# A graph layer and an attention layer on one core: attention and scores of a group of four samples as one block in every second step

## The chip, the cores and the metric

The kernel runs on one NeuronCore of a Trainium2 chip. Five engines run their own instruction streams and meet at semaphores: TensorE (PE; its weight loads are listed apart as PEld), VectorE (DVE), ScalarE (ACT), GpSimd (POOL), and SyncE (SP), which here issues the DMAs. The metric is device time in microseconds of one execution. Three executions gave 1952.86, 1950.43 and 1951.32 us, median 1951.32.

## The reference

The input `x` is 128 samples of 128 nodes by 512 features, and `adj` is a 128 x 128 matrix of weights. Cut to what matters (names shortened):

```python
# layer 0, per sample
A = adj @ x                       # with W1 = W2 = adj the difference C - A is the bias b alone
x = layernorm(x + max_n relu(A[:, n] + b))         # one number per node, added to its row
# layer 1, per sample: 8 heads of 64
q, k, v = split(x @ w_qkv)
p = softmax(where(adj == 0, -inf, q @ k.T / 8))
o = (p @ v) @ w_proj + b_proj
x = layernorm(x + o + layernorm(o) * gamma + beta)
```

All of it is float32. The only mask is `adj`, the same for all samples and heads.

## The kernel before

**Tiling.** The 128 samples are 64 pairs and 32 groups of four (`G = 4`). The products with the large weights are made per group, 512 tokens at once, as *units* (class `Unit`): `qk_unit(g, 0)` and `qk_unit(g, 1)` give the transposed queries and keys of two halves of the heads, `v_unit(g)` the values, `o_unit(g)` the output projection. A unit is a fast 2 x 2 block multiplication with seven products instead of eight: `product(i)` issues four fp32 matmuls of 128x128 by 128x256 (each is two MATMUL records in the trace, so a product is a row of x8), `snap(k)` copies bank 1 to SBUF on ACT, and `result(half, col)` adds a bank and a snap on DVE into the unit's output. `result(h, c)` reads bank 3 with snap 3 (1,1), bank 4 with snap 3 (1,0), bank 2 with snap 1 (0,0) and bank 3 with snap 2 (0,1). The sums of operands that the method needs run on POOL (`x_sums`, `o_sums`, `run_sums`).

**PSUM.** Eight banks, each one tag: b1 to b4 belong to the unit at work (products 1, 6, 7 share b1; 5 and 3 share b3; 2 has b2; 4 has b4); `po`, `pa`, `pss0`, `pss1` serve the attention, the scores and layer 0's product with `adj`.

**Per sample.** `scores(b)` (L396) makes eight small matmuls of 64 rows, even and odd heads into two banks. `softmax_max(b)` (L407) scales and masks each bank on DVE into a tile `s` and takes the negated maxima `nmax`. `softmax_exp` (L425) is one ACT activation per head with its sum. `softmax_div` and `prob_transpose` (L439, L447) run on DVE. `prob_write` (L457) sends the 32x32-transposed probabilities to DRAM, and `prob_read` (L466, four DMAs) fetches them back as the transposed tile `pT`. `attend(b)` (L482) makes eight small matmuls of 64 columns from `pT` and the values, and `attend_copy` (L496) takes the result to `oT` on ACT.

**The loop.** `for p in range(LAST)` (L810, `LAST = 60`) handles one pair of samples per step and two units per step: even steps (`ph == 0`) do `qk_unit(g + 1, 0)` and `o_unit(g - 1)`, odd ones `qk_unit(g + 1, 1)` and `v_unit(g + 1)`. Every step from the second on begins with `attend` of the two samples of the step before and `scores` of its own two, in one stretch of small matmuls between two units. Beside that, a step carries layer 0 for a later pair (`l0_norm`, `l0_transpose`, `l0_write`, `l0_read`, `l0_mm`, `l0_max`, `l0_add`), and the tails of earlier pairs (`tail_bias`, `tail_inner`, `tail_residual`, `tail_outer`, `tail_store`), whose row statistics `bn` computes on DVE (`one("o", ...)`, `one("z", ...)`, `one("y", ...)`) and `finish_stats` ends on POOL. After the loop the last four steps are written out by hand (from L983).

**What sets the order.** Every instruction is pinned (`pin = tc.keep_in_program_order`), so each engine executes its instructions in the order of the source; there is no planner. A tile's tag and `bufs` say how many buffers it rotates through: a new tile waits until the readers of the one whose buffer it takes are done. The SP queue issues DMAs in source order too, and one that has to wait holds those behind it.

Of the kernel before, what the change touches and what calls it, by code (L numbers as in the profile page):

```python
# [16 lines left out]
def kernel(  # L17
# [10 lines left out]
    out: bass.AP,  # L28
):


# [18 lines left out]
    H = 8  # L50
    HD = D // H
    KC = D // P
    G = 4
# [258 lines left out]
    def l0_transpose(q):  # L312

        xts[q] = sb.tile([P, Q, KC, 2, QS], F32, tag="xt", name=f"xt_{q}", bufs=2)
        for j in range(2):
            pin(
                nc.vector.transpose(  # L317
                    xts[q][:, :, :, j].rearrange("p q c b -> p c q b"),
                    xs[2 * q + j].rearrange("p (c q a) -> p c q a", c=KC, q=Q),
                )  # L320
            )
# [50 lines left out]
    def qk_unit(g, q):  # L372
        for h in range(2):
            qk[g, q, h] = sb.tile(
                [P, 2, 2, HT], F32, tag=f"qk{h}", name=f"qk_{g}_{q}_{h}", bufs=2 + h
            )
        out = {(h, c): qk[g, q, h][:, c] for h in range(2) for c in range(2)}
        return Unit(f"qk_{g}_{q}", x_lefts[g], weight_stationary(wqk, 2 * q * P), out)

    def v_unit(g):  # L380
        for h in range(2):
            vs[g, h] = sb.tile([P, 2, D], F32, tag="v", name=f"v_{g}_{h}", bufs=2)
        out = {(h, c): vs[g, h][:, :, ds(c * HE, HE)] for h in range(2) for c in range(2)}
        return Unit(f"v_{g}", x_lefts.pop(g), tokens_stationary(wv), out)
# [21 lines left out]

    def softmax_max(b):  # L407
        s = sb.tile([P, 2, NP, P], F32, tag="s", name=f"s_{b}", bufs=2)
        for par in range(2):
            pin(  # L410
                nc.vector.scalar_tensor_tensor(  # L411
                    s[:, par],
                    pss[b][par],
                    SCALE,
                    mask.unsqueeze(1).to_broadcast([P, NP, P]),
                    ALU.mult,
                    ALU.add,
                )
            )
        del pss[b]  # L420
        prob[b] = s.rearrange("p a h m -> p (a h) m")
        nmax[b] = small.tile([P, H], F32, tag="nmax", name=f"nmax_{b}")
        pin(nc.vector.tensor_reduce(nmax[b], prob[b], AX.X, ALU.max, negate=True))  # L423
# [42 lines left out]
    def prob_read(b):  # L466
        hop = hops.pop(b)
        pT[b] = sb.tile([P, Q, H, QS], F32, tag="pT", name=f"pT_{b}", bufs=2)
        for q in range(Q):
            pin(  # L470
                nc.sync.dma_start(
                    out=pT[b][ds(q * QS, QS)].rearrange("a i h b -> a i (h b)"),
                    in_=hop[:, :, q].rearrange("i a f -> a i f"),
                )
            )
# [144 lines left out]
    def z_tile(b):  # L620
        q, j = divmod(b, 2)
        tag, bufs = {58: ("xt", 2), 59: ("xt", 2), 60: ("z", 1), 61: ("qk0", 2)}.get(q, ("xs", 1))
        if tag == "xs":
# [182 lines left out]
    def tails(p):  # L806
        return [q if q >= 0 else None for q in (p - 3, p - 4, p - 5)]

    LAST = B // 2 - 4
    for p in range(LAST):  # L810
        g, ph = divmod(p, 2)
        a, b = 2 * p, 2 * p + 1
        first = v_unit(0) if p == 0 else qk_unit(g + 1, ph)
        n = p + 4 if p + 4 < B // 2 else None
        f = p + 5 if p + 5 < B // 2 else None
# [4 lines left out]
        def one(kind, src, q):  # L820
            for t in (2 * q, 2 * q + 1):
                bn(src[t], mv, len(keys))
                keys.append((kind, t))

        if p > 0:
            attend(a - 2)
            before.snap(3)
            attend_copy(a - 2)
            attend(b - 2, "pa")
            attend_copy(b - 2)  # L830
            scores(a)
            scores(b, ("po", "pa"))
        else:
            before.snap(3)
        before.result(1, 1)
        if ph == 0 and p > 0:
            run_sums(xsums[2:3])
        if ph == 0 and ta is not None:
            tail_bias(ta)
        if ph == 0 and g > 0:  # L840
            sums = o_sums(g - 1)
            run_sums(sums[:3])
        if n is not None and p > 0:
            for j in range(2):
                l0_norm(2 * n + j)
        if tb is not None:
            tail_inner(tb)
        if p > 0:
            softmax_max(a)
        before.result(1, 0)  # L850
        if p > 0:
            softmax_max(b)
            first.product(1)
            first.snap(1)
            first.product(2)
            softmax_exp(a)
        else:
            first.product(2)
            first.product(1)
            first.snap(1)  # L860
            for j in range(2):
                l0_norm(2 * n + j)
        first.result(0, 0)
        before.product(3)
        before.result(0, 1)
        if ph == 0 and p > 0:
            run_sums(xsums[3:])
        if ph == 0 and g > 0:
            run_sums(sums[3:])
        if tb is not None:  # L870
            tail_residual(tb)
        if n is not None:
            l0_transpose(n)
            l0_write(n)
            l0_beta(n)
        if ph == 1 and ta is not None:
            tail_bias(ta)
        first.product(6)
        if p == 0:
# [5 lines left out]
            softmax_exp(a)  # L885
        else:
            softmax_exp(b, range(4))
            first.snap(2)
            softmax_exp(b, range(4, H))
        first.product(5)  # L890
        first.product(4)
        first.product(7)
        if p == 0:
            first.snap(3)
            softmax_exp(b)
        softmax_div(a)
        prob_transpose(a)
        prob_write(a)
        if n is not None:
            l0_read(n)  # L900
        if p > 0:
            first.snap(3)
        else:
            first.result(1, 1)
            first.result(1, 0)
# [4 lines left out]
        prob_read(b)  # L910
        if p > 0:
            first.result(1, 1)
            first.result(1, 0)
        if ph == 1 and tb is not None:
            one("z", zs, tb)
        if ph == 0 and ta is not None:
            one("o", o_rows, ta)
        if f is not None:
            for j in range(2):
                l0_mm(2 * f + j, f"pss{j}")  # L920
        if to is not None:
            tail_outer(to)
            tail_store(to)
        if n is not None:
            l0_spill(n)
        if ta is not None:
# [11 lines left out]
        second.snap(1)  # L938
        if f is not None:
            for j in range(2):  # L940
                l0_max(2 * f + j)
                l0_add(2 * f + j)
        first.product(3)
        first.result(0, 1)
        if ph == 0 and tb is not None:
            one("z", zs, tb)
        if ph == 1 and ta is not None:
            one("o", o_rows, ta)
        second.product(6)
        second.snap(2)  # L950
        second.product(5)
        second.result(0, 0)
        second.product(4)
# [3 lines left out]
        if p == 1:  # L957
            weight_sums(wp, 0, HE)
            bd = const.tile([P, HE], F32, name="bd")
            tt(nc.gpsimd, bd, bp_bc[:, HE:], bp_bc[:, :HE], ALU.subtract)  # L960
        if f is not None:
            one("y", xs, f)
# [4 lines left out]
        before = second  # L967


# [14 lines left out]
    keys = []  # L984
    attend(L - 9)
    before.snap(3)
    attend_copy(L - 9)
    attend(L - 8, "pa")
    attend_copy(L - 8)
    scores(L - 7)  # L990
    scores(L - 6, po_pa)
    before.result(1, 1)
# [4 lines left out]
    tail_inner(LQ - 7)  # L997
    softmax_max(L - 7)
    before.result(1, 0)
    softmax_max(L - 6)  # L1000
    first.product(1)
    first.snap(1)
    first.product(2)
    softmax_exp(L - 7)
    first.result(0, 0)
    before.product(3)
    before.result(0, 1)
    run_sums(xsums[3:])
    run_sums(sums[3:])
    tail_residual(LQ - 7)  # L1010
    first.product(6)
    scores(L - 5)
    scores(L - 4, po_pa)
    softmax_exp(L - 6, range(4))
    first.snap(2)
    softmax_exp(L - 6, range(4, H))
    first.product(5)
# [3 lines left out]
    softmax_max(L - 5)  # L1021
    first.snap(3)
    prob_out(L - 6)
    first.result(1, 1)
    prob_read(L - 7)
# [30 lines left out]
    second.product(7)  # L1056
    prob_out(L - 4)

# [6 lines left out]
    attend(L - 6, "pa")  # L1065
    attend_copy(L - 6)
    prob_read(L - 5)
    prob_read(L - 4)
    before.result(1, 1)
    before.result(1, 0)  # L1070
    o_u.product(1)
# [16 lines left out]
    softmax_max(L - 3)  # L1088
    softmax_max(L - 2)
    o_u.product(6)  # L1090
    o_u.snap(2)
# [10 lines left out]
    o_u.result(1, 1)  # L1102
    o_u.result(1, 0)
    softmax_max(L - 1)
    stats("last_1", ("o", L - 9), ("o", L - 8))
# [7 lines left out]
    softmax_exp(L - 1, range(4, H))  # L1113
    v_u.relayed()
    softmax_max(L)
    for t in (L - 9, L - 8):
# [158 lines left out]
```

## Time and profile before

| what | value |
|---|---|
| profiled execution, device time | 1951.72 us |
| its span (first to last instruction) | 1949.8 us |
| PE busy | 1936.3 us, 99% of the span |
| DVE, POOL, ACT busy | 1564.1, 1293.1, 1063.7 us (80%, 66%, 55%) |
| PE clock granted | 0.999 |
| DMA | 341.74 MB, mean 175 GB/s |
| start of one step's small matmuls to the next | 29.97 us (1003.34 to 1033.31 to 1063.28) |

The page gives each engine's busy time, then the chain of work that ended last, followed back from the last instruction: at each step to what released it, or to the instruction before it on its engine. The timeline lists merged stretches of equal instructions of an engine: start, length, engine, line, operation, output and inputs, shapes, count, and in brackets an idle time before it and what ended it. The length runs from the first start to the last end; as matmuls are pipelined, an end lies up to 0.27 us (small ones) or 0.38 us (128x256) after the record's start, and the rate is read from starts.

### The profile page before, as it was taken

What the parts mean: (1) busy time and instruction counts of PE and PEld (TensorE: products, weight loads), DVE (VectorE), ACT (ScalarE), POOL (GpSimd) and SP (SyncE); (2) the same over time, 40 slices, a digit from 0 to 9 for tenths busy, and PEclk for the clock granted to TensorE, in tenths of its full rate; (3) what the DMA queues carried; (4) which work ended last, traced back from release to release, by engine and by line L of the source; (5) the groups of instructions that cost most, each with busy time, mean ns of one, the idle gap of its engine ahead of it and who ended that gap; (6) DMA issues with size and microseconds to landing.
All of it is one profiled execution on the core that took longest, in us unless ns stands there. A gap on an engine that the chain in (4) does not pass through costs nothing.

```text
span 1949.8 us, 33046 instructions
## 1 busy us (share of the span) xinstructions
PE 1936.3 (99%) x11541; PEld 1641.8 (84%) x11541; DVE 1564.1 (80%) x2515; ACT 1063.7 (55%) x3094; POOL 1293.1 (66%) x823
## 2 busy tenths in 40 slices
PE   9999999999999999999999999999999999999998
PEld 6888888888888888888888888888888888888885
DVE  7767878778778787787887877877878778778787
ACT  3444655555546555555465555554655555546566
POOL 6436766768667676667676676766767666767648
PEclk9999999999999999999999999999999999999999
DMA  7747566576576665766766757657667576675564
GB/s 221 176 119 192 141 186 176 161 205 159 167 195 159 187 176 167 199 157 171 203 152 183 182 160 199 163 166 195 157 185 191 156 195 164 166 206 152 157 226 141
DMA packets 444934, 341.74 MB, mean 175 GB/s; under 512 B 276832, under 2 KB 378336, under 8 KB 444768
## 3 DMA queue, kind: packets, MB, share of 16 engines
q1 hardware_dynamic: 444336, 338.85, 64.5%
q8 instruction: 91, 1.49, 0.3%
q10 hardware_dynamic: 432, 0.79, 0.1%
q14 instruction: 75, 0.61, 0.1%
HBM read 172.82 MB, written 166.72 MB: 174 GB/s over the span
## 4 chain that ended last, share of the span: by engine, by line
PE 94%; DVE 3%; POOL 1%; ACT 1%; issue 0%; POOLq 0%; ACTq 0%; DVEq 0%
PE b_qk L74 39%; PE b_v L74 19%; PE b_o L74 18%; PE pss L74 6%; PE po L74 6%; PE pa L74 5%; DVE st_mv_last L261 0%; POOL zl L77 0%; DVE s_x L77 0%; ACT s L430 0%; POOL s_o L77 0%; DVE amax L297 0%; PE idle L74 0%; DVE xt L317 0%; DVE mv_last L262 0%
## 5 line engine op out<-in xcount | busy, mean ns | idle before, releaser
L74 PE MATMUL b_qk<-s_x,wqk 128*128 128x256 f32 x2048 | 473.7, 380 | 1.0 <-DVE qk L77 0.7
L74 PEld LDWEIGHTS b_qk<-s_x,wqk 128*128 128x128 f32 x2048 | 389.8, 191 | 54.7 <-DVE qk L77 1.4
L430 ACT ACTIVATE s<-s,nmax 128x128 f32<-128x128 f32 x1024 | 396.0, 390 | 5.3 <-DVE nmax L423 5.3
L74 PE MATMUL b_qk<-x1T,wqk 128*128 128x256 f32 x1536 | 359.0, 384 | 1.1 <-DVE x1T L329 1.0
L74 PEld LDWEIGHTS b_qk<-x1T,wqk 128*128 128x128 f32 x1536 | 287.5, 190 | 45.3 <-POOL wqk L77 1.2
L77 POOL TENSOR_TENSOR z<-z,ga_bc 128x1024 f32<-128x1024 f32 x58 | 164.6, 2838 | 167.1 <-ACT z L284 167.1
L275 POOL TENSOR_SCALAR rs_mv<-mv 128x6 f32<-128x6 f32 (+2 forms) x61 | 14.7, 241 | 386.0 <-DVE mv L262 386.0
L77 DVE TENSOR_TENSOR s<-s,rec 128x1024 f32<-128x1024 f32 x128 | 252.6, 1973 | 4.4
L186 ACT COPY u_qk<-b_qk 128x512 f32<-128x512 f32 x192 | 112.3, 585 | 238.5 <-PE b_qk L74 237.5
L74 PE MATMUL b_v<-wv,s_x 128*128 128x256 f32 x1024 | 237.1, 380 | 0.0
L74 PE MATMUL b_o<-wp,s_o 128*128 128x256 f32 x992 | 229.6, 380 | 0.2 <-ACT u_o L186 0.2
L74 PEld LDWEIGHTS b_v<-wv,s_x 128*128 128x128 f32 x1024 | 195.0, 191 | 26.3 <-ACT u_v L186 0.4
L411 DVE SCALAR_TENSOR_TENSOR s<-pss,mask 128x512 f32<-128x512 f32 x256 | 164.4, 684 | 61.1 <-PE pss L74 60.9
L74 PEld LDWEIGHTS b_o<-wp,s_o 128*128 128x128 f32 x992 | 188.8, 191 | 25.8 <-issue 0.8
L77 DVE TENSOR_TENSOR qk<-b_qk,u_qk 128x512 f32<-128x512 f32 x256 | 168.0, 675 | 48.9 <-PE b_qk L74 44.5
L77 POOL TENSOR_TENSOR x<-x,be_bc 128x1024 f32<-128x1024 f32 x64 | 182.1, 2847 | 30.8 <-DVE rec L441 27.4
L430 ACT ACTIVATION_READ_ACCUMULATOR s<-s,nmax 128x1 f32 x1024 | 193.5, 189 | 0.0
L77 DVE TENSOR_TENSOR v<-b_v,u_v 128x512 f32<-128x512 f32 x127 | 86.2, 680 | 131.5 <-PE po L74 128.8
L186 ACT COPY u_o<-b_o 128x512 f32<-128x512 f32 x91 | 53.3, 585 | 239.6 <-PE b_o L74 239.6
L186 ACT COPY u_v<-b_v 128x512 f32<-128x512 f32 x95 | 55.6, 585 | 234.3 <-PE b_v L74 234.3
L74 PE MATMUL b_v<-wv,x1T 128*128 128x256 f32 x768 | 176.5, 380 | 0.0
L74 PEld LDWEIGHTS b_v<-wv,x1T 128*128 128x128 f32 x768 | 146.3, 191 | 31.8 <-issue 13.6
(130 smaller groups left out, 3402.9 us busy)
## 6 DMA issues: line engine op xcount, KB each, us to landing
hop<-pu SPq DMA_DIRECT2D x128, 512.0 KB, 3.6
pT<-hop SPq DMA_DIRECT2D x512, 128.0 KB, 3.6
spill<-x SPq DMA_DIRECT2D x64, 512.0 KB, 4.7
x<-in_x_dram SPq DMA_DIRECT2D x62, 512.0 KB, 4.2
xhop<-xt SPq DMA_DIRECT2D x248, 128.0 KB, 2.3
x1T<-xhop SPq DMA_DIRECT2D x248, 128.0 KB, 3.9
xr<-spill SPq DMA_DIRECT2D x59, 512.0 KB, 3.3
out_dram<-xr SPq DMA_DIRECT2D x58, 512.0 KB, 4.0
```

The lines of the kernel that those rows point to most:

```text
L74: pin(nc.tensor.matmul(*args, **kwargs))
L77: pin(eng.tensor_tensor(dst, a, b, op))
L186: pin(nc.scalar.copy(t, self.banks[1]))
L275: pin(nc.gpsimd.tensor_scalar(rs[:, :n], mv[:, :n, 1], EPS, None, ALU.add))
L411: nc.vector.scalar_tensor_tensor(s[:, par], pss[b][par], SCALE, mask.unsqueeze(1).to_broadcast([P, NP, P]), ALU.mult, ALU.add,)
L430: nc.scalar.activation(prob[b][:, i], prob[b][:, i], AF.Exp, bias=nmax[b][:, i : i + 1], accum_out=psums[b][:, i : i + 1],)
```

## The change

The change touches the loop's order and a few buffers; no instruction is added or removed on any engine.

- `group_block(old)` puts the attention of four samples (two in step 2) and the scores of the next four into one stretch at the start of each even step from step 2 on. Odd steps from 3 on have no such stretch. The four attentions use `po`, `pa`, `pss0`, `pss1`; the scores use b2 and b1, then b4 and `po`, then `pa` and `pss0`, then `pss1` and b2.
- `softmax_max` is split: `softmax_mask` does the masking, and can be called ahead. `group_mask` masks all four samples of a group in the even step, the last one's second bank first. The maxima of the third sample are taken at the end of the even step, those of the fourth early in the odd step.
- `v` has four buffers instead of two, `qk1` two instead of three, `xt` one instead of two (with one `xt` tile in `z`'s buffer). `s` and `pT`, two each before, share one tag with four.
- In odd steps the results of the unit before come ahead of most else on DVE, exponentials of the third sample's first half run first on ACT, and those of the fourth sample's second half after the unit's last snap.
- In even steps the maxima of layer 0 (`l0_first`) and the statistics move behind the unit's second snap, and `second.result(0, 0)` comes ahead of the statistics of `z`.
- In the hand-written end the first block takes four attentions and four scores as well, `prob_out(L - 4)` moves into the next block, and the last two samples are masked into spare room of the weight buffer.

```diff
-        xts[q] = sb.tile([P, Q, KC, 2, QS], F32, tag="xt", name=f"xt_{q}", bufs=2)
+        tag = "z" if q == 3 else "xt"
+        xts[q] = sb.tile([P, Q, KC, 2, QS], F32, tag=tag, name=f"xt_{q}", bufs=1)
...
-                [P, 2, 2, HT], F32, tag=f"qk{h}", name=f"qk_{g}_{q}_{h}", bufs=2 + h
+                [P, 2, 2, HT], F32, tag=f"qk{h}", name=f"qk_{g}_{q}_{h}", bufs=2
...
-            vs[g, h] = sb.tile([P, 2, D], F32, tag="v", name=f"v_{g}_{h}", bufs=2)
+            vs[g, h] = sb.tile([P, 2, D], F32, tag="v", name=f"v_{g}_{h}", bufs=4)
...
-    def softmax_max(b):
-        s = sb.tile([P, 2, NP, P], F32, tag="s", name=f"s_{b}", bufs=2)
-        for par in range(2):
+    def softmax_mask(b, order=(0, 1), place=None):
+        s = place or sb.tile([P, 2, NP, P], F32, tag="s", name=f"s_{b}", bufs=4)
+        for par in order:
...
+    def softmax_max(b):
+        if b in pss:
+            softmax_mask(b)
...
-        pT[b] = sb.tile([P, Q, H, QS], F32, tag="pT", name=f"pT_{b}", bufs=2)
+        pT[b] = sb.tile([P, Q, H, QS], F32, tag="s", name=f"pT_{b}", bufs=4)
...
+    def group_block(old):
+        a = old[-1] + 1
+        free = ["po", "pa", "pss0", "pss1"]
+        for t in old:
+            attend(t, free[0])
+            attend_copy(t)
+            free.append(free.pop(0))
+        banks = ("b2", "b1"), ("b4", free[0]), (free[1], free[2]), (free[3], "b2")
+        for k in range(G):
+            scores(a + k, banks[k])
+
+    def group_mask(a):
+        softmax_mask(a)
+        softmax_mask(a + 1)
+        softmax_max(a)
+        softmax_mask(a + 2)
+        softmax_mask(a + 3, (1, 0))
...
+        elif ph == 0:
+            group_block(range(2 if p == 2 else a - G, a))
+            before.result(1, 1)
...
+            before.result(1, 0)
+            group_mask(a)
+            softmax_max(b)
+            first.product(1)
+            first.snap(1)
+            softmax_exp(a)
+            before.product(3)
+            first.product(2)
+            before.result(0, 1)
+            first.result(0, 0)
...
         else:
+            softmax_exp(a, range(4))
+            before.result(1, 1)
+            before.result(1, 0)
+            softmax_max(b)
             first.product(2)
             first.product(1)
             first.snap(1)
...
+            first.snap(2)
+            if ph:
+                softmax_exp(a, range(4, H))
+                softmax_exp(b, range(4))
+            else:
+                softmax_exp(b)
...
-        if p == 0:
+        if p == 0 or ph and p > 1:
             first.snap(3)
-            softmax_exp(b)
+            softmax_exp(b, range(4 if p else 0, H))
...
         second.product(6)
         second.snap(2)
+        if p > 1:
+            if ph == 0:
+                one("o", o_rows, ta)
+            l0_first()
         second.product(5)
-        second.result(0, 0)
+        if ph == 0:
+            second.result(0, 0)
+            one("z", zs, tb)
+        else:
+            one("z", zs, tb)
+            one("o", o_rows, ta)
+            second.result(0, 0)
...
+        if ph == 0 and 1 < p < LAST - 1:
+            softmax_max(a + 2)
```

More of the change, by code (lines that the diff above doesn't have):

```diff
@@ L621, in z_tile @@
         q, j = divmod(b, 2)
-        tag, bufs = {58: ("xt", 2), 59: ("xt", 2), 60: ("z", 1), 61: ("qk0", 2)}.get(q, ("xs", 1))
+        tag, bufs = {58: ("xt", 1), 59: ("x", 2), 60: ("z", 1), 61: ("qk0", 2)}.get(q, ("xs", 1))
         if tag == "xs":
@@ L813 @@
         first = v_unit(0) if p == 0 else qk_unit(g + 1, ph)
-        n = p + 4 if p + 4 < B // 2 else None
+        n = p + 4
         f = p + 5 if p + 5 < B // 2 else None
@@ L820, in one, with l0_first @@
         def one(kind, src, q):
-            for t in (2 * q, 2 * q + 1):
+            for t in (2 * q, 2 * q + 1) if q is not None else ():
                 bn(src[t], mv, len(keys))
                 keys.append((kind, t))
[L825 to L830, printed above, removed]
+        def l0_first():
+            if f is not None:
+                for t in (2 * f, 2 * f + 1):
+                    l0_max(t)
+                    l0_add(t)
+        before.snap(3)
+        if p == 0:
+            before.result(1, 1)
[3 more added lines that the diff above has]
+            first.snap(1)
+            for j in range(2):
+                l0_norm(2 * n + j)
+            first.result(0, 0)
+            before.product(3)
+            before.result(0, 1)
+        elif p == 1:
+            for t, tag in ((0, "po"), (1, "pa")):
+                attend(t, tag)
+                attend_copy(t)
             scores(a)
             scores(b, ("po", "pa"))
[L833 to L843, printed above, removed]
+            before.result(1, 1)
             for j in range(2):
                 l0_norm(2 * n + j)
-        if tb is not None:
-            tail_inner(tb)
-        if p > 0:
             softmax_max(a)
-        before.result(1, 0)
-        if p > 0:
+            before.result(1, 0)
             softmax_max(b)
@@ L856 @@
             softmax_exp(a)
-        else:
+            first.result(0, 0)
+            before.product(3)
+            before.result(0, 1)
+        elif ph == 0:
+            group_block(range(2 if p == 2 else a - G, a))
+            before.result(1, 1)
+            run_sums(xsums[2:3])
+            if ta is not None:
+                tail_bias(ta)
+            sums = o_sums(g - 1)
+            run_sums(sums[:3])
+            for j in range(2):
+                l0_norm(2 * n + j)
+            if tb is not None:
+                tail_inner(tb)
+            before.result(1, 0)
+            group_mask(a)
+            softmax_max(b)
+            first.product(1)
+            first.snap(1)
+            softmax_exp(a)
+            before.product(3)
+            first.product(2)
+            before.result(0, 1)
+            first.result(0, 0)
+            run_sums(xsums[3:])
+            run_sums(sums[3:])
+        else:
+            softmax_exp(a, range(4))
+            before.result(1, 1)
+            before.result(1, 0)
+            softmax_max(b)
             first.product(2)
@@ L860 @@
             first.snap(1)
+            if tb is not None:
+                tail_inner(tb)
             for j in range(2):
                 l0_norm(2 * n + j)
[L863 to L869, printed above, removed]
+            first.result(0, 0)
+            before.product(3)
+            before.result(0, 1)
         if tb is not None:
             tail_residual(tb)
[L872 to L875, printed above, removed]
+        l0_transpose(n)
+        l0_write(n)
+        l0_beta(n)
         if ph == 1 and ta is not None:
@@ L885 @@
             softmax_exp(a)
-        else:
+        elif p == 1:
             softmax_exp(b, range(4))
@@ L898 @@
         prob_write(a)
-        if n is not None:
-            l0_read(n)
-        if p > 0:
+        l0_read(n)
+        if p == 1 or ph == 0 and p > 1:
             first.snap(3)
-        else:
+        if p != 1:
             first.result(1, 1)
@@ L910 @@
         prob_read(b)
-        if p > 0:
+        if p == 1:
             first.result(1, 1)
             first.result(1, 0)
[L914 to L917, printed above, removed]
         if f is not None:
@@ L923 @@
             tail_store(to)
-        if n is not None:
-            l0_spill(n)
+        l0_spill(n)
         if ta is not None:
@@ L938 @@
         second.snap(1)
[L939 to L942, printed above, removed]
+        if p < 2:
+            l0_first()
         first.product(3)
         first.result(0, 1)
[L945 to L948, printed above, removed]
         second.product(6)
         second.snap(2)
+        if p > 1:
+            if ph == 0:
+                one("o", o_rows, ta)
+            l0_first()
         second.product(5)
-        second.result(0, 0)
+        if ph == 0:
+            second.result(0, 0)
+            one("z", zs, tb)
+        else:
+            one("z", zs, tb)
+            one("o", o_rows, ta)
+            second.result(0, 0)
         second.product(4)
@@ L984 @@
     keys = []
-    attend(L - 9)
     before.snap(3)
[L987 to L991, printed above, removed]
+    group_block(range(L - 11, L - 7))
     before.result(1, 1)
@@ L997 @@
     tail_inner(LQ - 7)
-    softmax_max(L - 7)
     before.result(1, 0)
+    group_mask(L - 7)
     softmax_max(L - 6)
@@ L1002 @@
     first.snap(1)
+    before.product(3)
     first.product(2)
     softmax_exp(L - 7)
+    before.result(0, 1)
     first.result(0, 0)
-    before.product(3)
-    before.result(0, 1)
     run_sums(xsums[3:])
@@ L1011 @@
     first.product(6)
-    scores(L - 5)
-    scores(L - 4, po_pa)
-    softmax_exp(L - 6, range(4))
     first.snap(2)
-    softmax_exp(L - 6, range(4, H))
+    softmax_exp(L - 6)
     first.product(5)
@@ L1022 @@
     first.snap(3)
+    first.result(1, 1)
     prob_out(L - 6)
-    first.result(1, 1)
     prob_read(L - 7)
@@ L1056 @@
     second.product(7)
-    prob_out(L - 4)
     before, o_u, v_u = second, o_unit(NG - 3), v_unit(NG - 1)
@@ L1066 @@
     attend_copy(L - 6)
+    before.result(1, 1)
+    before.result(1, 0)
+    prob_out(L - 4)
     prob_read(L - 5)
     prob_read(L - 4)
-    before.result(1, 1)
-    before.result(1, 0)
     o_u.product(1)
@@ L1089 @@
     softmax_max(L - 2)
+    place_of = {
+        b: room[:, ds(2 * q, 2)].rearrange("p a (h m) -> p a h m", m=P)
+        for b, q in ((L - 1, 3), (L, 4))
+    }
     o_u.product(6)
@@ L1103 @@
     o_u.result(1, 0)
+    softmax_mask(L - 1, place=place_of[L - 1])
     softmax_max(L - 1)
@@ L1114 @@
     v_u.relayed()
+    softmax_mask(L, place=place_of[L])
     softmax_max(L)
```

## The prediction

> **What bounds the kernel now.** I read the page's busy rows and chain first, then the timeline of one step, then the waits.
>
> ```profile
> span 1949.8 us, 33046 instructions
> PE 1936.3 (99%) x11541; PEld 1641.8 (84%) x11541; DVE 1564.1 (80%) x2515; ACT 1063.7 (55%) x3094; POOL 1293.1 (66%) x823
> ...
> PE 94%; DVE 3%; POOL 1%; ACT 1%; issue 0%; POOLq 0%; ACTq 0%; DVEq 0%
> ```
>
> TensorE is the path. Its steps start exactly 29.97 us apart, 57 times in a row, so no other engine delays it inside the loop. A gain must therefore come from TensorE's own time. Busy time hides where that is lost; starts show it:
>
> ```profile
> 1001.52 1.89 PE L74 MATMUL b_v<-wv,s_x 128*128 128x256 f32 x8
> 1003.34 1.97 PE L74 MATMUL po<-pT,v 128*64 128x128 f32 x32
> 1005.24 2.06 PE L74 MATMUL pss<-qk 64*128 64x128 f32 x32
> 1007.23 3.72 PE L74 MATMUL b_qk<-x1T,wqk 128*128 128x256 f32 x16
> 1010.78 1.89 PE L74 MATMUL b_v<-wv,s_x 128*128 128x256 f32 x8
> 1012.51 3.62 PE L74 MATMUL b_qk<-s_x,wqk 128*128 128x256 f32 x16
> 1015.96 1.89 PE L74 MATMUL b_qk<-x1T,wqk 128*128 128x256 f32 x8
> ```
>
> Sixteen unit records from 1012.51 to 1015.96 take 3.45 us, 0.216 each. The sixteen just after the scores take 3.55.
>
> ```profile
> 1003.72 1.15 PE L74 MATMUL po<-pT,v 128*64 128x128 f32 x18
> 1006.57 0.72 PE L74 MATMUL pss<-qk 64*128 64x128 f32 x10
> ```
>
> These are narrow windows inside the two small stretches. The records run in pairs 7 ns apart. Less one record's 0.27 us, the first shows 8 pairs' spacing in 0.88, or 0.110 us a pair, the second 4 in 0.45, or 0.112.
>
> ```profile
> PEld po L74 <- issue: 18.0, 54, 0.8
> PEld pss L74 <- issue: 11.6, 64, 0.3
> ```
>
> In the weight queue's waits, the load of the first small weights sits idle at nearly every switch, though no semaphore holds it.
>
> **The merged block, priced.** From 1001.52 to 1010.78 is 9.26 us. At the steady rates its 24 unit records take 5.18, 16 attention pairs 1.76 and 16 score pairs 1.79, together 8.73. So entering, changing over and leaving costs 0.53 us a stretch. Start by start it is 0.545, since each switch delays two intervals: into attention 309 ns for 216, then 153 for 103; to scores 203 for 103, then 207 for 105; back 201 for 105, then 320 for 216. The order of both programs shows that switches from attention to scores fall from 60 to 31. The work inside moves to the even step at the same rate, so 29 odd steps give back 29 x 0.545 = **15.8 us**. The last section's separate scores, at 1851.77, join its first block and save 93 + 102 + 96 + 104 ns = 0.4. Sum **16.2 us**.
>
> [...] The rows say 0.18 us a switch, because the second interval is late too. I take the rows.
>
> [...] Against it: the 55 ns a record are flat to the end of today's stretch. Also, TensorE's semaphore instruction ahead of the second attention runs 22 ns after the stretch begins, 16 records ahead of use; the one ahead of the product `s4_o`, in an odd step, runs 22 ns after the units resume, again 16 records ahead. The lead isn't eaten, so I price this at nothing. Two more attentions in a row add four such instructions, 110 ns apart, against a lead of 0.88 us.
>
> **Does TensorE get everything in time?** With 0 at the first attention record, the even step is: scores at 3.67, units at 7.45, then `first` 1 to 9.28, old 3 to 11.0, 2 to 12.7, 6, 5, 4 and 7 to 19.6, `pa` to 21.4, then `o` 1, 2, `first` 3 (24.8 to 26.5), `o` 6, 5, 4, 7 to 33.4. The odd step runs 2, 1, then old 3 at 36.9, 6, 5, 4, 7 to 45.5, `pa`, `v` to 59.3. The pair is 59.40 us instead of 59.94.
>
> *Even step, DVE.* `result(1,1)` and `(1,0)` end near 2.5; b4 is wanted at 4.6. Today they wait for the attention because `v` has two buffers (DVE `v` <- PE `po`, 128.8 us); with four that wait goes, and the old snap is then last, at 0.75. Masks come next:
>
> ```profile
> 1006.43 1.29 DVE L411 SCALAR_TENSOR_TENSOR s<-pss,mask 128x512 f32<-128x512 f32 x2 [0.32 <-PE pss L74]
> 1007.76 1.22 DVE L423 TENSOR_REDUCE nmax<-s 128x8 f32<-128x1024 f32 x1
> ```
>
> A mask begins 1.19 after its scores begin, follows the last at 0.61, and a maximum takes 1.14. So four masks from 4.86, the maximum from 7.3, three masks from 8.4: the one that frees b2 ends at 10.3, and product 2 wants b2 at 11.0. Behind that product the whole unit would queue; cover 0.7. b2's first use is masked by 5.5, wanted at 6.5.
>
> *End of the even step, DVE.* This is the tightest place:
>
> ```profile
> 1026.51 0.69 DVE L77 TENSOR_TENSOR qk<-b_qk,u_qk 128x512 f32<-128x512 f32 x1 [0.87 <-PE b_qk L74]
> ...
> 1031.04 0.17 DVE L273 TENSOR_SCALAR sh_mv<-mv 128x6 f32<-128x6 f32 x1
> ```
>
> `qk`'s last result starts 1.92 after product 3 does, at 26.7. Behind it now stand statistics of `o` (1.61), `l0_first` (1.69), `o`'s result (0.6), statistics of `z` (1.59), the moved maximum (1.14), statistics of `y` with the shift (1.9), and only then `result(1,1)` (0.66), which frees b3. Each is from this timeline, start to start; with `qk`'s own 0.61 they sum to 9.8, ending at 36.5. TensorE wants b3 at 36.9, so 0.4 of cover. A near row: today the second sample's scores start about 0.3 us after the ACT copy that frees their bank, without a stall. So 0.4 is enough. If the chain were longer, each 0.1 us beyond the cover would cost 2.9 us over 29 pairs.
>
> *Odd step.* `result(0,1)` ends at 39.5 against 40.4 for product 5; ACT's snaps all keep over half a microsecond. The fourth sample's last exponentials end at 47.9, its division and transpose at 51.3, and SP issues its write at about 51.7, with nothing queued ahead of it by then:
>
> ```profile
> 1021.57 0.75 SPq L460 DMA_DIRECT2D hop<-pu  x1
> 1022.42 5.20 SPq L471 DMA_DIRECT2D pT<-hop  x8
> ```
>
> From that write's issue to the landing of the last `pT` part the trace has a median of 9.0 us, so 60.7. The fourth attention starts at 59.4 + 2.7 = 62.1; cover 1.4. The even step's `pT` have a step to spare.
>
> *The rest, at nothing.* POOL's work is the same; its statistics begin about 3.5 us later against the block, yet `s2_x` is ready by 6 for product 6 at 12.7. SP's even step is issued some 7 us later (the second transpose ends at 25.0, not 18.0), so `x` lands near 41, wanted at 45.5. One `xt` buffer is written a step after its last DMA; `qk1`'s two are rewritten after the block has read them; each mask takes the buffer that its attention has just read. If any cover failed, the price would be the same 29 per unit of lateness. In the written-out end, the last `qk` unit's `result(0,1)` may be some 0.4 us late, once; moved DVE work there can return as much. Bounds minus 1 and plus 1, taken as 0.
>
> The sum: 1951.7 - 16.2 = **1935.5 us** for the profiled execution. The median, 1951.3, lies 0.4 below that execution and would give 1935.1; I keep 1935.5, for a stall or two.
>
> **The rivals.**
> *A: part is given back to DVE* (chance 0.22). The chain to b3, or the masks to b2, runs over by 0.1 to 0.4 us. For: seven items in a row with 0.4 of cover. Against: their durations spread by under 0.03 us. At 0.2 late: 1935.5 + 5.8 = 1941.3.
> *B: the switch's second interval or the issue remains* (0.09)[...] Against: the second intervals sit only beside switches.
> *C: slower* (0.07): the fourth sample's transposed probabilities arrive late, because they now start some 6 us later against the next stretch (today's write is issued 11 us ahead of it). TensorE has nothing else queued, so lateness is paid in full, 29 times. It decides from 2.0 us over the median, a landing 11.0 us after issue: 0.55 late eats the gain. At 11.4, 1935.5 + 29 x 0.9 = 1961.6. For: landings up to 10.6 occur in the loop. Against: none there reaches 11.
> *Forecast* (0.62): 1933.5 to 1938.5.
>
> **How the numbers follow.** About 0.2% is what a measurement of this kernel can tell from no change, 3.9 us. [...] The range 1933 to 1943 takes in the forecast and most of A.
>
> **What would show it.** Odd steps without a stretch of small matmuls; stretches of 64 attention and 64 score records taking 3.67 and 3.79 us from start to start; these starts 59.40 us apart. In the waits, TensorE's "issue" idle ahead of `po` and `pss` should halve. Wrong would be: `b_qk` or `b_o` waiting for DVE once a pair (A), spacing that grows inside the block (B), `po` waiting for a DMA (C).

## The result and the profile after

The changed kernel takes 1935.54 us (median of four, 1935.32 to 1935.88) against 1950.88 for the kernel before on the same chip: a ratio of 0.992, 95% interval 0.9903 to 0.9937. The forecast was 1935.5. The profiled spans fell from 1949.8 to 1934.1 us, by 15.8 before rounding.

The page of the changed kernel, the rows that answer to those shown of before:

```profile
span 1934.1 us, 33370 instructions
PE 1920.0 (99%) x11541; PEld 1638.0 (85%) x11541; DVE 1595.1 (82%) x2515; ACT 1055.3 (55%) x3094; POOL 1289.0 (67%) x823
...
PE 94%; DVE 4%; POOL 1%; ACT 1%; issue 0%; POOLq 0%; ACTq 0%; DVEq 0%
```

TensorE has the same 11541 records, is as busy in share, and still makes 94% of the chain. The instructions that do work are as many as before on every engine. The 324 more in all (33370 for 33046) are semaphore instructions: 177 more on ACT, 120 on DVE, 57 on SP, 29 fewer on TensorE, 1 on POOL. Busy time alone doesn't say what got better. The starts do; the timeline of TensorE around one block of the changed kernel (start, length, what, count):

```profile
1050.97 1.89 PE L75 MATMUL b_v<-wv,s_x 128*128 128x256 f32 x8
1052.79 3.71 PE L75 MATMUL po<-pT,v 128*64 128x128 f32 x64
1056.43 3.84 PE L75 MATMUL pss<-qk 64*128 64x128 f32 x64
1060.21 1.99 PE L75 MATMUL b_qk<-x1T,wqk 128*128 128x256 f32 x8
1062.04 1.89 PE L75 MATMUL b_v<-wv,s_x 128*128 128x256 f32 x8
```

From the last unit product at 1050.97 to the second one after the block at 1062.04 are 11.07 us. At the rates of the kernel before, 16 unit records are 3.45, 32 attention pairs 3.51 and 32 score pairs 3.58, together 10.54: the block costs its 0.53 us once, for twice the work. Attention to scores takes 3.64 us and scores to unit 3.78, where 3.67 and 3.79 were forecast. Record by record the switches are those of before (309, 153, then 202, 207, then 202, 320 ns), and the pairs stay 109 and 112 ns apart to the end. In the loop the late intervals stand where the weights' shape changes. Where the product's alone changes there is none: between two units, and from a unit to layer 0's product with `adj` and on (the same 128x128 weights, but 512 columns for 256), the intervals are 216 or 429 ns.

The waits of the weight loads (total us, times, longest):

```profile
PEld po L75 <- issue: 10.9, 32, 0.8
PEld pss L75 <- issue: 6.3, 34, 0.3
```

Before they were 18.0 and 11.6. They have about halved, as the number of switches has. They are a sign and not the price: the same view has 30.0 us ahead of `pa`, where TensorE's records show no delay (216 and then 429 ns).

The account closes. In the loop, the starts of steps 2 and 60 are 1719.35 us apart instead of 1736.54; 1.76 of that is the attention of two samples that now stands in step 60's own block, and 0.4 is given back in step 59 (below), so the loop's switches gained 15.8. From step 60's start to the end it takes 110.48 instead of 109.06: the 1.76 moved there less the 0.4 of the merged scores. The start, 104.2 us up to step 2, is unchanged in the two profiles.

### The profile page after: what moved, and what is told of

It reads as the page before. It is cut to its first block, busy times and chain, and to the rows that moved or that the text cites. A ratio compares the mean times of both kernels' runs of the same rounds, so it can differ in the third digit from the quotient of the medians.

```text
span 1934.1 us, 33370 instructions
## 1 busy us (share of the span) xinstructions
PE 1920.0 (99%) x11541; PEld 1638.0 (85%) x11541; DVE 1595.1 (82%) x2515; ACT 1055.3 (55%) x3094; POOL 1289.0 (67%) x823
## 4 chain that ended last, share of the span: by engine, by line
PE 94%; DVE 4%; POOL 1%; ACT 1%; issue 0%; POOLq 0%; ACTq 0%; DVEq 0%
PE b_qk L75 39%; PE b_v L75 19%; PE b_o L75 19%; PE pss L75 6%; PE po L75 6%; PE pa L75 5%; DVE st_mv_last L262 0%; POOL zl L78 0%; DVE s_x L78 0%; ACT s L437 0%; POOL s_o L78 0%; DVE amax L298 0%; DVE s L78 0%; PE idle L75 0%; DVE pu L458 0%
## 5 line engine op out<-in xcount | busy, mean ns | idle before, releaser
L437 ACT ACTIVATE s<-s,nmax 128x128 f32<-128x128 f32 x1008 | 390.3, 391 | 3.4 <-DVE nmax L430 3.4
L78 DVE TENSOR_TENSOR s<-s,rec 128x1024 f32<-128x1024 f32 x126 | 279.8, 2221 | 4.3
L414 DVE SCALAR_TENSOR_TENSOR s<-pss,mask 128x512 f32<-128x512 f32 x252 | 156.5, 683 | 76.3 <-PE pss L75 76.3
L75 PE MATMUL b_o<-wp,oT 128*128 128x256 f32 x744 | 171.1, 379 | 0.3 <-ACT b_o L552 0.3
```

Of the source, the lines that this page charges most:

```text
L75: pin(nc.tensor.matmul(*args, **kwargs))
L78: pin(eng.tensor_tensor(dst, a, b, op))
L414: nc.vector.scalar_tensor_tensor(s[:, par], pss[b][par], SCALE, mask.unsqueeze(1).to_broadcast([P, NP, P]), ALU.mult, ALU.add,)
L437: nc.scalar.activation(prob[b][:, i], prob[b][:, i], AF.Exp, bias=nmax[b][:, i : i + 1], accum_out=psums[b][:, i : i + 1],)
```

## Experiments

### More switches and nothing else

A block of the changed kernel, with one sample's scores moved between two attentions:

```diff
-        for t in old:
+        for i, t in enumerate(old):
             attend(t, free[0])
             attend_copy(t)
             free.append(free.pop(0))
+            if i == 1:
+                scores(a, ("b2", "b1"))
...
-        for k in range(G):
+        for k in range(1, G):
             scores(a + k, banks[k])
```

> The changed kernel, but in each block the first sample's scores stand between the second and the third attention, so that a block has two switches more (scores to attention and back) and nothing else differs. 29 blocks have four attentions. If a switch costs what the starts show (two late intervals, 0.14 to 0.20 us together), a block gains 0.34 to 0.40 us and the time is 1935.5 + 10 to 12 = 1945.5 to 1947.5. [...] If the gain came from something else than the switches (the order on DVE, the buffers), 1935.5.

Measured: 1945.84 us, ratio to the kernel before 0.9972 (0.9962 to 0.9982). Its TensorE timeline around one block:

```profile
1057.56 1.97 PE L75 MATMUL po<-pT,v 128*64 128x128 f32 x32
1059.46 1.16 PE L75 MATMUL pss<-qk 64*128 64x128 f32 x16
1060.55 1.97 PE L75 MATMUL po<-pT,v 128*64 128x128 f32 x32
1062.45 2.95 PE L75 MATMUL pss<-qk 64*128 64x128 f32 x48
1065.33 1.99 PE L75 MATMUL b_qk<-x1T,wqk 128*128 128x256 f32 x8
```

The block goes from 7.42 us (1052.79 to 1060.21) to 7.77 (1057.56 to 1065.33) with the same records. A pair of steps takes 59.742 us instead of 59.393: 0.349 for two switches. The next run alternates once more, as below; the scores of the samples behind them follow as in the changed kernel:

```diff
+            if i in (1, 2) and len(old) == G:
+                scores(a + i - 1, (("b2", "b1"), ("b4", "po"))[i - 1])
...
-        for k in range(G):
+        for k in range(2 if len(old) == G else 0, G):
```

> As the run with two switches more, but the second sample's scores stand alone too: four switches more in 29 blocks. By the switch price twice the loss, 1935.5 + 20 to 23.2 = 1955.5 to 1958.7, about 4 to 7 us above the kernel before; the spacing inside the short stretches stays 0.110 and 0.112 us a pair. [...]

Measured: 1955.76 us, ratio 1.002 (1.0011 to 1.0029). A pair takes 60.091 us, 0.698 more than the changed kernel's: twice 0.349. Four more switches a block eat the gain and a little over, with every buffer, bank and DVE order of the change but the scores' place kept. So the loss and the gain are proportional to the switches: 0.349 us for two more, 0.698 for four, 0.545 for the three of a stretch, about 0.18 each. These runs vary the switches between the two small shapes; those from and to a unit were not varied by themselves, and have their price from the starts and from the pair of steps as a whole (59.94 to 59.393 us).

### Is issue a limit in a long block?

```diff
-            attend(t, free[0])
+            attend(t, free[0], 2)
...
-        for pr in range(NP):
+        for pr in list(range(NP)) * times:
```

The attentions of the block are computed twice over. If issue held up a long stretch, the pairs would stand further apart at its end than at its beginning.

> The changed kernel with the small matmuls of each attention in the block issued twice into the same bank, so that a block has 192 records in a row instead of 128. [...] the pairs stay 0.110 us apart to the end and 29 blocks gain 32 pairs, 3.51 us each (the block of step 2 half of it): 1935.5 + 103.5 = 2039. [...]

Measured: 2039.12 us. The timeline of that run:

```profile
1043.23 7.21 PE L75 MATMUL po<-pT,v 128*64 128x128 f32 x128
1050.36 3.84 PE L75 MATMUL pss<-qk 64*128 64x128 f32 x64
```

128 records from 1043.23 to 1050.36 are 64 pairs in 7.13 us. With the slow first interval and the switch out of them taken off, the pairs stand 0.109 us apart, the last like the first. The 64 score records behind them take 3.78 us (1050.36 to 1054.14), as in the changed kernel. So over 192 small records in a row the spacing doesn't grow, and issue shows no price.

### The buffers alone

The kernel before, with one more buffer for `v` in the room of one of `xt` (whose edit is that of the change):

```diff
-            vs[g, h] = sb.tile([P, 2, D], F32, tag="v", name=f"v_{g}_{h}", bufs=2)
+            vs[g, h] = sb.tile([P, 2, D], F32, tag="v", name=f"v_{g}_{h}", bufs=3)
...
```

> The kernel before with three buffers for v and one for xt (its second one's room), order untouched. DVE's waits of v for the attention (128.8 us in 30 waits) vanish. If they were off the path, the time stays 1951 within 0.2%. If part of the change's gain came from these buffers, it is faster by that part.

Measured: 1950.75 us, ratio 0.9997 (0.9989 to 1.0006). DVE's waits in the kernel before:

```profile
DVE v L77 <- PE po L74: 128.8, 30, 5.9
DVE s L411 <- PE pss L74: 60.9, 62, 2.1
```

And in that run:

```profile
DVE s L412 <- PE pss L74: 99.9, 62, 2.1
DVE o L77 <- ACT u_o L186: 90.0, 30, 4.8
DVE v L77 <- ACT u_v L186: 89.8, 30, 4.6
```

The 128.8 us of `v` waiting for `po`, the largest wait of DVE before, are gone. In their place DVE waits 89.8 us for ACT's copy, and 39 more for the scores: the same idle time under other names. The wait of an engine off the path was worth nothing.

### How much cover has DVE?

Two runs lengthen the chain ahead of bank 3 in the odd steps. First a maximum that nobody reads:

```diff
             softmax_exp(a, range(4))
+            again = small.tile([P, H], F32, tag="again", name=f"again_{p}")
+            pin(nc.vector.tensor_reduce(again[:, :4], prob[b][:, :4], AX.X, ALU.max, negate=True))
             before.result(1, 1)
```

> The changed kernel with one more DVE maximum (half a sample, into a tile nobody reads) ahead of result(1,1) at the start of each odd step from 3 on, about 0.6 us. In the changed kernel's trace that result ends 0.5 us before TensorE's product 3 begins. If that is the cover, 0.1 to 0.2 us of lateness remains in 29 odd steps: 1935.5 + 3 to 6 = 1938.5 to 1941.5. If the cover were really larger (slack elsewhere takes it up), 1935.5; if there is none, 1935.5 + 17 = 1953.

Measured: 1944.13 us, 8.6 above the changed kernel and more than expected. Then the order of statistics ahead of results:

```diff
             softmax_exp(a, range(4))
+            softmax_max(b)
             before.result(1, 1)
             before.result(1, 0)
-            softmax_max(b)
```

> The changed kernel with softmax_max(b) put ahead of result(1,1) and result(1,0) in the odd steps, as an order with statistics ahead of results would have it: the result that frees b3 comes 1.12 us later. Cover 0.5, so TensorE waits 0.6 to 0.75 us in each of 29 odd steps: 1935.5 + 17 to 22 = 1952.5 to 1957.5, the whole gain. If DVE's order doesn't matter, 1935.5.

Measured: 1960.34 us, ratio 1.0045 (1.003 to 1.006): slower than the kernel before, and above the expected range too. First the changed kernel: DVE, and TensorE's product 3 that wants the bank:

```profile
1029.11 1.28 DVE L78 TENSOR_TENSOR o<-b_o,u_o 128x512 f32<-128x512 f32 x2
...
1030.26 1.89 PE L75 MATMUL b_o<-wp,s_o 128*128 128x256 f32 x8
```

The two results are 0.60 apart, so the first, which frees bank 3, ends at 1029.80, 0.46 ahead of 1030.26. Now the run with the order undone:

```profile
981.43 1.21 DVE L430 TENSOR_REDUCE nmax<-s 128x8 f32<-128x1024 f32 x1
982.56 1.28 DVE L78 TENSOR_TENSOR o<-b_o,u_o 128x512 f32<-128x512 f32 x2
...
979.13 3.62 PE L75 MATMUL b_qk<-x1T,wqk 128*128 128x256 f32 x16
983.39 1.97 PE L75 MATMUL b_o<-wp,s_o 128*128 128x256 f32 x8 [0.64 <-POOL sh_mv L78]
```

The first result ends near 983.24 and TensorE starts at 983.39. The hand-over takes 0.15 us, so the real cover is 0.31, not 0.46. Undelayed, product 3 would start 3.45 after 979.13, at 982.58; it is 0.81 late, and 1.12 of delay less 0.31 of cover is 0.81. The small dose agrees: 0.60 less 0.31 is 0.29, and its product is 0.274 late. The period of a pair grows by a little more, 0.883 and 0.349, because the second interval after the wait is 0.075 late too. (27 periods of 0.349 are 9.4 us; that the medians differ by 8.6 fits the start before step 2, which is 1.1 shorter in this profile and varies by as much in others.) The view names POOL's `sh_mv` as what ended the wait. That is a releaser inferred from semaphores. In the median pair `sh_mv` ends 37.64 us after the block's start in all three kernels, and in the changed one that is 0.78 after product 3 has begun. So it doesn't hold the product; DVE's result, which moves with the dose, does. With the maxima ahead of the results in odd steps, the merged block loses more than it gains.

### How much cover have the transposed probabilities?

In the odd steps the two `prob_read` calls move on the SP queue, behind the store of the output and the spill:

```diff
-        prob_read(a)
-        prob_read(b)
+        late = ph == 1 and p > 1
+        if not late:
+            prob_read(a)
+            prob_read(b)
...
         l0_spill(n)
+        if late:
+            prob_read(a)
+            prob_read(b)
```

> The changed kernel with the odd steps' prob_read DMAs issued on SP behind the output's store and the spill, about 1.0 us later. The last part lands at 61.5 instead of 60.45 after the block's start, the fourth attention starts at 62.1: still in time, 1935.5. If the cover is smaller than the trace says, up to 29 x 1 = 1964.

Measured: 1988.27 us. A clear miss. TensorE's waits in that run:

```profile
PE po L75 <- DMA pT<-hop: 40.4, 33, 2.2
```

Medians over its pairs, from the block's start: the reads are issued from -5.51 us (changed kernel: -6.84), the last part lands at 4.03 (1.17), and the fourth attention starts at 4.26 (2.67). The first read is issued only 1.33 later, but the landing is 2.86 later. A megabyte of store and spill now moves ahead of the reads and beside them; the eight issues are spread over 4.88 us instead of 3.93, and the last read lands 4.54 after its issue instead of 3.87. The cover in the median pair is 2.67 less 1.17 less a hand-over of 0.23 (0.13 in the next run), or 1.27 us, and 1.59 of lateness is left. The same edit with the reads behind the reload of `xr` as well, which waits on the SP queue for the store to land (`SPq L586 <- DMA out_dram<-xr` in the changed kernel: 198.2 us in 57 waits):

> As the run with the reads behind the spill, but behind the reload of xr too, which waits until the output's store has landed (4 to 4.5 us). The reads then start near 57.2 and the last part lands near 65.2, 3.1 us after the fourth attention could start. If lateness is paid in full, once per pair of steps, 1935.5 + 29 x 3.1 = 2025 (2005 to 2045 as the landing varies). If TensorE's queue or later slack takes part of it up, less.

Measured: 2078.46 us, 143 above the changed kernel instead of 90. The last part lands at 6.10, 4.93 later than in the changed kernel, and a pair of steps takes 4.97 us longer on average. That isn't the fourth attention's lateness alone, which is 3.56. Two windows of one block show the rest; the columns are the window's length, busy time of the PE records (and their number), the granted clock, the DMA share and GB/s:

```profile
418.20:421.40 3.20, 3.01 (x26) 0.50 0.18 65
421.60:424.00 2.40, 2.40 (x48) 1.00 0.03 7
```

The fourth attention starts at 418.39, after a second wait for `pT`. From 418.2 to 421.4 TensorE is granted half of its clock, and from 421.6 all of it again. So the fourth attention takes 1.91 us instead of 0.97, and the 64 score records 4.33 (420.30 to 424.63) instead of 3.78. The trace has such a fall, of 3.4 or 6.8 us, in 19 of 26 pairs. In the 7 pairs without one, a pair is longer by the lateness of its fourth attention and 0.05 us more; in the 19 with one, by 1.8 more on average (0.5 to 3.0). The run before has a fall in 2 of its 26 pairs, and 0.05 in the other 24. Lateness is paid in full, and where the clock falls there is a surcharge.

### The gap that was left

In the changed kernel one record at 1818.2 us starts 0.3 us late, and its stretch of 16 records takes 4.02 us instead of 3.62. It was first put down to bank 3 behind `result(1, 0)` in the written-out end:

```diff
     softmax_max(L - 4)
-    first.result(1, 0)
...
     first.result(0, 1)
+    first.result(1, 0)
```

> The changed kernel with first.result(1, 0) of the last qk unit moved behind first.result(0, 1) in the written-out end. In the changed kernel's trace a b_v or b_qk record there (at 1818.2) starts 0.3 us late, because bank 3 is read behind result(1, 0). If that is the cause, the gap goes and the span is 0.3 us shorter, too little for the median to show: 1935.2 against 1935.5. If the gap has another cause, it stays.

Measured: 1936.21 us, and a gap of the same size (502 ns where 216 is the rule) stays. That theory fell. The block of step 60 starts only at 1823.6, so the gap lies in step 59, the last of the loop. It has no `l0_mm` between its units, and DVE is in the transpose until 1817.6, so its result, which frees bank 3, ends only at 1818.1:

```diff
-        second.product(5)
+        second.product(5 if f is not None else 4)
...
-        second.product(4)
+        second.product(4 if f is not None else 5)
```

> The changed kernel with v's product 4 ahead of product 5 in the loop's last step alone. That step has no layer-0 products between the units, so TensorE comes to product 5 about 1.7 us sooner than in the other odd steps, and DVE's result(0, 1), which frees b3, stands behind the fourth sample's division and transpose until 1818.1. If that is the gap of 0.3 us at 1818.2, it goes and the span falls by 0.3 us (a median near 1935.2, too little to tell from 1935.5). If the gap stays, its cause is another one.

Measured: 1934.34 us (1934.22 to 1934.51), ratio to the kernel before 0.9914 (0.9901 to 0.9928). Its TensorE timeline in step 59:

```profile
1815.15 1.89 PE L75 MATMUL b_v<-wv,s_x 128*128 128x256 f32 x8
1816.87 1.89 PE L75 MATMUL b_v<-wv,x1T 128*128 128x256 f32 x8
1818.60 3.62 PE L75 MATMUL b_v<-wv,s_x 128*128 128x256 f32 x16
1822.15 3.06 PE L75 MATMUL po<-pT,v 128*64 128x128 f32 x52
```

Products now follow each other at 1.73 us, and steps 2 to 60 take 1718.94 us, 0.40 less than in the changed kernel. That part is the edit's. The median fell by 1.2, but 1.0 of the profiles' difference lies in the start before step 2 (103.2 against 104.2 us), which the edit doesn't touch; another profile of this study has 105.1 there. By its interval the version isn't told apart from the changed kernel.

## Why the prediction was right

**The price of a switch** held: 0.545 us a stretch, 29 times, and 0.4 at the end. The loop's pair of steps was forecast at 59.40 us and takes 59.393. The runs with two and four more switches give it alone, 0.349 for one from scores to attention and one back. The forecast leaned on the second late interval of each switch: the first ones alone (93, 100 and 96 ns) would give 0.289 us a stretch, 8.4 for 29.

**That the total is off by only 0.04** is luck in part. The forecast took 16.2 us off the one profiled execution, 1951.72. The medians on one chip differ by 15.3 and the profiled spans by 15.8. The gain was forecast a little too large, from a start a little too high.

**Issue at nothing** held, and the run with attentions twice over shows it past the length that the change needs: a record takes 55 ns there as well, to the end.

**The buffers at nothing** held (0.9997).

**The covers** were right in sign. The chain to bank 3 was forecast to end 0.4 ahead of its use and ends 0.46 ahead. What the forecast left out is the hand-over from DVE to TensorE, 0.15, so its "each 0.1 us beyond the cover would cost 2.9" holds only from 0.31 on, with the 0.075 of the second interval on top: rival A had less cover against it than stated. The division of probabilities became slower, 2.22 us on average instead of 1.97, where no change was forecast: DVE is 31 us busier with the same instructions. TensorE lost nothing by it, as the 59.393 show, but rival C's cover did.

**Rival C** stayed away, but with less room than stated. The fourth sample's exponentials end at 47.9 as forecast; its division takes 2.62 us where the forecast's sum has about 1.9, so the write is issued 7.3 us ahead of the block and not 7.7. The last part lands 8.5 us after that issue, not 9.0. The two misses cancel, so that the landing came out as forecast is luck. The cover is 1.27 in the median pair, not 1.4, because the hand-over takes 0.23, and 0.57 in the worst. Two DMAs put ahead on the same queue turned it into a loss of 53 us. "Paid in full" was right, to 0.05 us, as long as the clock stays up.

**The end** was taken as nothing with bounds of plus and minus 1. With the moved work and the 0.4 of the scores counted, the written-out end lost 0.06. Step 59 lost 0.4 that the forecast hadn't seen: it had looked for a late `result(0,1)` one step later.

## What to carry to other kernels

Where TensorE is busy all the time, read the spacing of record starts around every change of tile shape. Here each change of the weights' shape cost two late intervals, 0.18 us together, that TensorE's busy time hid, and putting equal shapes together paid because each other engine's results still came in time. Before merging, list for every bank what must be done ahead of its next use, and keep a hand-over in each cover (here 0.15 us from DVE to TensorE, 0.23 from a DMA). And leave a DMA's place in its queue alone unless you know what will move beside it: the reads of two samples, moved behind a store and a spill, cost 53 us here.

## What the hardware showed that was not expected

- The second interval of a switch is late by 50 ns where the new weights have 64 columns (attention), and by 102 to 104 where they have 128 (scores, units). In the traces before and after, the weight load that belongs to it begins 55 ns after the first load of the new shape for 64 columns, and 108 for 128. An interval of 320 ns for 216 also follows waits between units, with no change of shape (516 and then 320 ns at 1817.7 in the changed kernel). What makes it late was not tried.
- In 19 of 26 pairs of the run with the latest reads, after idle stretches of 0.5 to 3.3 us, mostly two close together, TensorE's granted clock fell to 0.5 and was back at 1.00 after 3.4 or 6.8 us. In the other 7 it did not fall, though the fourth attention was 3.4 us late there on average (3.7 in the others); what decides was not tried.
- The division on DVE (`s<-s,rec`, 128x1024, SBUF to SBUF) takes 1.225 us where POOL is idle beside it (3 of 128 before the change, 6 of 126 after), and mostly between 1.5 and 2.8 where POOL works beside it. Which of POOL's instructions it meets isn't all: beside the same two (`o<-o,bp_bc` and `x<-x,be_bc`) it takes 1.90 before and 2.64 after the change. So a new order on the two engines changed it; what sets the time was not tried.
